# Table loads issued by GpSimd, smaller X tiles and regrouped products in an edge-gated graph kernel

## Chip, core and metric

The kernel runs on one NeuronCore of a Trainium2 chip. The metric is device time in microseconds (us) of one execution; the time of a kernel is the median of its runs.

## What is computed

One gated graph layer over 16 batches of 1024 nodes with 256 features and a sparse 1024 x 1024 adjacency matrix (0.4% of the pairs, made symmetric, and the diagonal):

```python
pre_u = einsum('bud,dk->buk', h, W1[:d]);  pre_v = einsum('bvd,dk->bvk', h, W1[d:])
S = sigmoid(einsum('buvk,ko->buvo', relu(pre_u[:,:,None] + pre_v[:,None] + b1), W2)[...,0] + b2[0])
a_t = einsum('buv,bud->bvd', S * A, h);     m_t = einsum('uv,bud->bvd', A, h) * h
z   = beta1*h + beta2*(a_t @ Wa + ba) + beta3*(m_t @ Wm + bm)
```

## The kernel before

**Pieces and blocks.** Only the edges are worked on. The 1024 targets v are cut into 8 tiles of 128, the 16 batches into 4 groups of 4; a *block* k is one target tile of one group, 32 blocks in all. A block has two windows of 64 targets, and each window five *pieces* of 128 edges: 320 pieces, numbered n, ten to a block. The place of a piece in its block is s = n mod 10. For each piece GpSimd (POOL) gathers 128 rows of 8 KB from a table in DRAM (`fetch`, L474): the first half of a row is pre_u of one source node for four batches, the second half its h. The gathers go into eight places (`fetched0` to `fetched7`); a place is free again when the piece's last product has read it, so about eight gathers are the whole lead.

**One step n** of the main loop (L844) does, in the order in which each engine gets its instructions: evict the last pair of pieces from PSUM (`pair_end`, L634, tile `ev`); expand the target side of piece n+2 by a product with a 0/1 matrix (`expand`, L573, tile `pc`, reading `X`); the block's own products (`products`); in even steps the aggregation of pieces n-2 and n-1 (`aggregate`, L626, tile `acc`), the two gathers that this frees room for, and some small gathers of edge weights (`val`, L348); then VectorE (DVE) adds (`add`, L603) and makes the gate's dot products (`gate`, L610), and ScalarE (ACT) makes the sigmoid (L613) and the weighted edge matrix `left` (L581, L617).

**Products of a block**, by step s: `halves` of the next block (L400 with w_v, L437 to L444; the target side X in a high and a low part); `turn_over` (L648, `LT`: the aggregated rows are transposed, once per window, and multiplied by h in `times_h`, L665); `block_end` of the block before (L676, L684, L688; `z`, L691, written out at L693); and `rows` (L400 with w_u, L416, `tab`, written to the table at L420), which makes table rows for a later group, in the steps listed by `plan` (L748 to L750).

**Loads.** `load_hT` (L389) loads the transposed h of one tile and group (512 KB) and is issued by SyncE (SP) 14 steps ahead (`AHEAD`) of its first use, if one of the 10 (later 13) places for it is free. `copy_h` (L394) copies h of the same rows, 512 KB from DRAM to the table in DRAM; in the main loop ACT issues it. SP also issues the writes of `tab` and `z`. During the first ten blocks the edge lists of tiles 4 to 7 are still being made (`lists`, L214 to L341): POOL loads a 512 KB tile `key` (L216) and DVE works on it from L224 on, in small instructions between the others; `start_list` says in which step each list begins, and `piece_of` how many steps pass after its load.

**What sets the order.** The program's own order is kept on each engine (a manual schedule); the framework puts in semaphore waits. DMAs share eight completion semaphores for those of SP and ACT together (shown as DMAHW0 to DMAHW7) and eight for those of POOL (DMASW0 to DMASW7), used in turn: a DMA waits on its engine until the DMA before it on the same semaphore has landed.

Of the kernel before, what the change touches and what calls it, by code (L numbers as in the profile page):

```python
# [17 lines left out]
def kernel(  # L18
# [364 lines left out]
    def drop_hT(k):  # L383
        hT_free.append(hTs.pop(k))
# [22 lines left out]
    def rows(k, tab=None):  # L407

        g, nt = k
        for h in range(2):  # L410
            step = yield
            c = slice(2 * h * D, (2 * h + 2) * D)
            p = small("p")
            half_product(p, hTs[k], w_u, h, False)
            t = big.tile([P, 2 * D], FP, name=f"tab{h}", bufs=1) if tab is None else tab[:, c]
            nc.scalar.copy(t, p)  # L416
            if h == 1 and k in again:
                drop_hT(k)
            if tab is None:
                after(step + 1, lambda t=t, c=c: nc.sync.dma_start(table[g][nt * P:(nt + 1) * P, c], t))  # L420
        if tab is not None:
            after(step + 1, lambda: nc.sync.dma_start(table[g][nt * P:(nt + 1) * P, :GD], tab))
# [5 lines left out]
    def halves(k):  # L428
        X = cuts[k] = big.tile([P, NW, GD], FR, name="X")
        low = one.tile([P, GD], FP, name="low")  # L430
        for h in range(2):
            step = yield
            c = slice(2 * h * D, (2 * h + 2) * D)
            p = small("p")
            add_row(p, b1_p)
            half_product(p, hTs[order[k]], w_v, h, True)
            nc.scalar.copy(X[:, 0, c], p)  # L437
            nc.scalar.copy(low[:, c], p)
        after(step + (2 if k else 1), lambda: nc.vector.tensor_tensor(low, low, X[:, 0, :].bitcast(FP), ALU.subtract))
        yield  # L440
        nc.scalar.copy(X[W:, 1, :], X[W:, 0, :].bitcast(FP))
        for w in range(NW):
            yield
            nc.scalar.copy(X[(1 - w) * W:(2 - w) * W, w, :], low[w * W:(w + 1) * W])  # L444
# [19 lines left out]
    EVS = 4  # L464
# [103 lines left out]
    def expand(n):  # L568
        k, g, vt, w, j = where(n)
        pcs[n] = psc.tile([P, GD], FP, name="pc")  # L570
        for h in range(2):
            c = slice(2 * h * D, (2 * h + 2) * D)
            nc.tensor.matmul(pcs[n][:, c], marks[n // TW][:, j * P:(j + 1) * P], cuts[k][:, w, c],  # L573
                             start=True, stop=True)
# [95 lines left out]
    def block_end(k):  # L670
# [6 lines left out]
        for h in range(2):  # L677
            for i, wt in ((1, w_a), (0, w_m)):
                step = yield
                if i:  # L680
                    pz = small("pz")
                    for bb in range(2):
                        for e in range(DC):
                            nc.tensor.matmul(pz[:, bb * D + e * P:bb * D + (e + 1) * P], hT[:, 2 * h + bb, e, :], ident,  # L684
                                             is_transpose=True, start=(bb == 0 and e == 0), stop=True, skip_group_check=True)
                for bb in range(2):
                    for c in range(DC):
                        nc.tensor.matmul(pz[:, bb * D:(bb + 1) * D], LT[:, 2 * h + bb, i if bb else 1 - i, c, :], wt[:, c, :],  # L688
                                         start=False, stop=True, skip_group_check=True)
            o = big.tile([P, 2, D], FP, name=f"z{h}", bufs=1)  # L690
# [5 lines left out]
        drop_hT(order[k])  # L696
# [42 lines left out]
    start_list = dict(zip((7, 18, 48, 86), range(EARLY, NT)))  # L739
# [8 lines left out]
    plan(turn[NT:], ((2, 4), (8, 9), (10, 14), (19, 20), (24, 29), (30, 34), (39, 40), (44, 48)))  # L748
    for g, first in ((2, 60), (3, 140)):
        plan([(g, vt) for vt in range(NT)], ((first + 9 + 10 * i, first + 14 + 10 * i) for i in range(NT)))  # L750
# [21 lines left out]
    def products(n, k, s):  # L772
# [238 lines left out]
```

## Time and profile before

| | |
|---|---|
| median of 3 runs | 1106.19 us (1101.87 to 1107.52) |
| the profiled execution, own time | 1100.63 us |
| its span, first to last instruction | 1098.8 us |
| busy of the span | PE 91%, DVE 89%, ACT 79%, POOL 42% |
| DMA: moved, mean rate | 375.00 MB, 341 GB/s |
| share of the 16 DMA engines by queue | POOL's (q0) 72.2%, SP's (q1) 16.7%, ACT's (q10) 3.6% |
| mean granted TensorE clock | 0.958 |

A row of the profile names a line of the kernel, an engine, and what is written and read (out<-in). "Idle before" is the time an engine stood still ahead of an instruction, and what ended it. The DMA share of a stretch is the time that packets took, as a share of 16 engines; packets of several queues can overlap on one engine, so it may be a little over 1.

### The profile page before, as it was taken

The numbers are of one execution on the slowest core, as the hardware profiler recorded it, in microseconds if no ns is written. First come the engines' busy times: TensorE is split into PE (matmuls) and PEld (weight loads), VectorE is DVE, ScalarE is ACT, GpSimd is POOL, SyncE is SP. The second block draws the span as 40 slices with busy tenths as digits, with TensorE's granted clock in tenths as the row PEclk, the third lists the DMA queues.
The fourth block names the chain that finished last, engine by engine and source line by source line (L and its number), as shares of the span: only waits on it lengthen the run. The fifth ranks groups of instructions, "written<-read, shape, count | busy, mean of one in ns | idle before, by whom it ended". The sixth has DMA issues, their size and how long they took to land.

```text
span 1098.8 us, 21630 instructions
## 1 busy us (share of the span) xinstructions
PE 997.1 (91%) x6377; PEld 721.6 (66%) x6377; DVE 977.8 (89%) x3392; ACT 869.7 (79%) x2712; POOL 466.9 (42%) x471
## 2 busy tenths in 40 slices
PE   7858889697999989996999997999999999999986
PEld 6635667475677757774777775777776666666654
DVE  8859989597999899995999996999999999999992
ACT  3437778486888978884988877988989999999972
POOL 2756766455357324651334332433333333333320
PEclk9968989799999999997999998999999999999998
DMA  9999999689999989998999998999999999999981
GB/s 285 329 383 349 367 329 368 221 305 350 348 342 357 380 330 369 379 383 289 360 377 377 395 361 287 377 365 387 353 363 360 364 347 343 357 365 349 359 311 32
DMA packets 133118, 375.00 MB, mean 341 GB/s; under 512 B 17680, under 2 KB 87824, under 8 KB 96784
## 3 DMA queue, kind: packets, MB, share of 16 engines
q0 software_dynamic: 50544, 301.16, 72.2%
q1 hardware_dynamic: 69152, 59.26, 16.7%
q10 hardware_dynamic: 13296, 13.11, 3.6%
q8 instruction: 53, 0.87, 0.3%
q14 instruction: 73, 0.60, 0.1%
HBM read 377.53 MB, written 50.33 MB: 389 GB/s over the span
## 4 chain that ended last, share of the span: by engine, by line
PE 52%; DMA 22%; DVE 11%; ACT 11%; issue 3%; POOL 1%; ACTq 0%; POOLq 0%; DVEq 0%; SPq 0%
PE misc L688 13%; PE misc L400 13%; PE acc L626 11%; PE pc L573 9%; DMA table<-tab 8%; DMA hT<-in_xT_dram 5%; DVE fetched L610 4%; DMA fetched<-table,uidx 4%; DVE fetched L603 3%; DMA key<-in_adjT_dram 3%; PE misc L648 3%; ACT left L617 2%; ACT LT L650 2%; PE misc L684 2%; ACT gt L613 1%
## 5 line engine op out<-in xcount | busy, mean ns | idle before, releaser
L474 POOL DMA_INDIRECT fetched<-table,uidx x320 | 344.7, 1077 | 538.7 <-PE acc L626 404.4
L610 DVE SCALAR_TENSOR_TENSOR fetched<-fetched,w_b 128x256 f32<-128x256 f32 x1280 | 474.4, 416 | 6.9 <-ACT gt L613 6.9
L603 DVE TENSOR_TENSOR fetched<-fetched,pc 128x1024 f32<-128x1024 f32 x320 | 387.6, 1211 | 67.7 <-PE pc L573 49.3
L617 ACT ACTIVATE left<-left,gt 128x16 f32<-128x16 f32 x1280 | 285.1, 296 | 0.0
L573 PE MATMUL pc<-X,mark 128*128 128x512 f32 x640 | 248.0, 470 | 29.3 <-DVE fetched L603 29.3
L626 PE MATMUL acc<-fetched,left 128*32 128x256 f32 x2560 | 228.4, 397 | 48.4 <-ACT left L617 28.7
L626 PEld LDWEIGHTS acc<-fetched,left 128*32 128x32 f32 x2560 | 93.4, 110 | 153.8 <-ACT left L617 71.6
L573 PEld LDWEIGHTS pc<-X,mark 128*128 128x128 f32 x640 | 107.2, 193 | 108.7 <-issue 51.8
L613 ACT ACTIVATE gt<-sc,b_b 128x4 f32<-128x4 f32 x320 | 96.3, 301 | 59.8 <-DVE fetched L610 47.2
L400 PE MATMUL misc<-w_u,hT 128*128 128x256 f32 x512 | 124.7, 392 | 6.1 <-DMA hT<-in_xT_dram 6.1
L400 PE MATMUL misc<-w_v,hT 128*128 128x256 f32 x512 | 122.6, 383 | 0.0
L688 PE MATMUL misc<-w_a,LT 128*128 128x256 f32 x496 | 121.4, 389 | 0.0
L688 PE MATMUL misc<-w_m,LT 128*128 128x256 f32 x496 | 117.4, 379 | 0.0
L400 PEld LDWEIGHTS misc<-w_u,hT 128*128 128x128 f32 x512 | 101.0, 198 | 22.5 <-DMA w_u<-in_W_dram 6.0
L400 PEld LDWEIGHTS misc<-w_v,hT 128*128 128x128 f32 x512 | 98.3, 192 | 15.9
L688 PEld LDWEIGHTS misc<-w_m,LT 128*128 128x128 f32 x496 | 93.7, 189 | 15.0 <-issue 0.4
L348 POOL DMA_INDIRECT val<-in_adjT_dram,vidx x80 | 88.4, 1105 | 31.8 <-issue 17.8
L688 PEld LDWEIGHTS misc<-w_a,LT 128*128 128x128 f32 x496 | 92.9, 198 | 10.7
L581 ACT ACTIVATE left<-onehot,val 128x32 f32<-128x32 bf16 x320 | 99.3, 310 | 0.0
L610 DVE DVE_READ_ACCUMULATOR fetched<-fetched,w_b 128x1 f32 x1280 | 98.9, 77 | 0.0
L634 ACT COPY ev<-acc 128x512 f32<-128x512 f32 x160 | 90.8, 568 | 5.7 <-PE acc L626 5.7
L437 ACT CAST X<-misc 128x512 fp32r<-128x512 f32 x64 | 37.4, 585 | 66.4 <-PE misc L400 66.2
(134 smaller groups left out, 936.3 us busy)
## 6 DMA issues: line engine op xcount, KB each, us to landing
hT<-in_xT_dram SPq DMA_DIRECT2D x35, 512.0 KB, 17.4
out_dram<-z SPq DMA_DIRECT2D x62, 256.0 KB, 10.5
table<-in_x_dram ACTq DMA_DIRECT2D x24, 512.0 KB, 15.3
table<-tab SPq DMA_DIRECT2D x48, 256.0 KB, 15.5
fetched<-table,uidx POOLq DMA_INDIRECT x320, 9.7
table<-in_x_dram SPq DMA_DIRECT2D x8, 512.0 KB, 11.8
table<-fetched SPq DMA_DIRECT2D x8, 512.0 KB, 11.9
fetched<-in_adjT_dram SPq DMA_DIRECT2D x4, 512.0 KB
```

Source lines behind the costliest of these rows:

```text
L348: nc.gpsimd.indirect_dma_start(out=val[:, i, j:j + 1], out_offset=None, in_=adj_flat, in_offset=bass.IndirectOffsetOnAxis(ap=vidx[:, i, j: ...
L400: nc.tensor.matmul(p[:, bb * D:(bb + 1) * D], hT[:, 2 * h + bb, i, :], wt[:, i, :], start=(i == 0 and not begun), stop=(i == DC - 1), skip ...
L474: nc.gpsimd.indirect_dma_start(out=fetched[at_slot[n]], out_offset=None, in_=table[g], in_offset=bass.IndirectOffsetOnAxis(ap=uidx[:, vt * ...
L573: nc.tensor.matmul(pcs[n][:, c], marks[n // TW][:, j * P:(j + 1) * P], cuts[k][:, w, c], start=True, stop=True)
L581: nc.scalar.activation(lefts[n][:, 1::GB, :], onehot[:, vt * NW + w, j, :].unsqueeze(1).to_broadcast([P, GB // 2, V]), AF.Copy, scale=val[ ...
L603: nc.vector.tensor_tensor(t, t, pcs.pop(n), ALU.add)
L610: nc.vector.scalar_tensor_tensor(t[:, b, :], t[:, b, :], 0.0, w2_b, ALU.max, ALU.mult, accum_out=sc[:, b:b + 1])
L613: nc.scalar.activation(gt, sc, AF.Sigmoid, bias=b2_b)
L617: nc.scalar.activation(lefts[n][:, 2 * b, :], lefts[n][:, 1 + b // 2 * GB, :], AF.Copy, scale=gt[:, b:b + 1])
L626: nc.tensor.matmul(accs[i][b * 2 * V:(b + 1) * 2 * V, r, :], left[:, 2 * b - b % 2:2 * b - b % 2 + 2].rearrange("p k v -> p (k v)"), f[:, ...
L634: nc.scalar.copy(evs[i], accs.pop(i))
L688: nc.tensor.matmul(pz[:, bb * D:(bb + 1) * D], LT[:, 2 * h + bb, i if bb else 1 - i, c, :], wt[:, c, :], start=False, stop=True, skip_grou ...
```

## The change

- **Issuers.** In the main loop the loads of hT and the copies of h are issued by POOL (in `made_rows`), no longer by SP and ACT. 26 loads and 24 copies move; the loads ahead of the main loop stay where they were.
- **X** is two tiles of 64 targets' use each (`X[0]`, `X[1]`, 4 KB a partition), out of three places, instead of one tile of 8 KB in two places. The second is taken when it is first written.
- **tab** has two places for each half of the rows instead of one; **z** three places for both halves together instead of one each; **ev** three places instead of four (`EVS`).
- **Places of hT** are given back one step later (`drop_hT` with a step).
- **Steps.** Rows of groups 2 and 3 are made at s = 9 and s = 0 instead of 9 and 4, and some of group 1 move by one step; `block_end` runs in steps 4 to 7 instead of 5 to 8, and makes the product with w_a first, then the transposes of h and the product with w_m into the same PSUM tile; the first `turn_over` of a block is at s = 8 instead of 9.
- **Lists.** A list's work begins eight steps after its load instead of four, and lists 5 to 7 start four steps sooner (14, 44, 82 instead of 18, 48, 86).

```diff
-            t = big.tile([P, 2 * D], FP, name=f"tab{h}", bufs=1) if tab is None else tab[:, c]
+            t = big.tile([P, 2 * D], FP, name=f"tab{h}") if tab is None else tab[:, c]
...
-        X = cuts[k] = big.tile([P, NW, GD], FR, name="X")
+        X = cuts[k] = [big.tile([P, GD], FR, name="X", bufs=3)]
...
-        nc.scalar.copy(X[W:, 1, :], X[W:, 0, :].bitcast(FP))
+        X.append(big.tile([P, GD], FR, name="X", bufs=3))
+        nc.scalar.copy(X[1][W:], X[0][W:].bitcast(FP))
...
-    EVS = 4
+    EVS = 3
...
-            r[1:] = said not in ("slot", "step"), n + {"load": 4, "wait": 2, "slot": 1, "step": 1}.get(said, 0)
+            r[1:] = said not in ("slot", "step"), n + {"load": 8, "wait": 2, "slot": 1, "step": 1}.get(said, 0)
...
                 if i:
                     pz = small("pz")
+                else:
                     for bb in range(2):
                         for e in range(DC):
...
-                                             is_transpose=True, start=(bb == 0 and e == 0), stop=True, skip_group_check=True)
+                                             is_transpose=True, start=False, stop=True, skip_group_check=True)
...
-            o = big.tile([P, 2, D], FP, name=f"z{h}", bufs=1)
+            o = big.tile([P, 2, D], FP, name="z", bufs=3)
...
-        drop_hT(order[k])
+        drop_hT(order[k], step + 1)
...
-    start_list = dict(zip((7, 18, 48, 86), range(EARLY, NT)))
+    start_list = dict(zip((7, 14, 44, 82), range(EARLY, NT)))
...
-        plan([(g, vt) for vt in range(NT)], ((first + 9 + 10 * i, first + 14 + 10 * i) for i in range(NT)))
+        plan([(g, vt) for vt in range(NT)], ((first + 9 + 10 * i, first + 10 + 10 * i) for i in range(NT)))
...
-                load_hT(k)
+                load_hT(k, nc.gpsimd)
             if k not in begun:
-                copy_h(k)
+                copy_h(k, nc.gpsimd)
...
-        if s in (4, 5, 6, 7, 8) and 0 < k < BS:
+        if s in (4, 5, 6, 7) and 0 < k < BS:
             if s == 4:
                 ending = block_end(k - 1)
                 next(ending)
+                go(ending, n)
             go(ending, n)
...
-            if s == 9 and k < BS - 1 or s == 8 and k == BS - 1:
+            if s == 8 and k < BS:
```

On ACT, before, step 125 (s = 5 of block 12; `table_62` is the table of group 2): the copy of h, L394, stands between the work on X and the gate of the step, and waits for the DMA before it on its semaphore.

```order
L634 COPY ev_5797<-acc 128x512 [waits PE_49]
L506 CAST mark<-whose 128x640 [waits DMASW7_49,DMASW0_49]
L441 CAST X<-X 64x1024
L394 DMA table_62<-in_x_dram 128x4x256 [waits DMAHW4_49]
L613 ACTIVATE gt<-sc,b_b 128x4 [waits DVE_49]
L581 ACTIVATE left<-onehot,val 128x2x16 [waits DMASW5_49]
L617 ACTIVATE left<-left,gt 128x16 [waits Activation_49]
```

The same step on ACT now: the copy is gone, and the eviction of z has come one step sooner.

```order
L639 COPY ev_5816<-acc 128x512 [waits PE_49]
L511 CAST mark<-whose 128x640 [waits DMASW1_49,DMASW0_49]
L446 CAST X<-X 64x1024
L697 COPY z<-misc 128x512 [waits DMAHW4_49,PE_49]
L618 ACTIVATE gt<-sc,b_b 128x4 [waits DVE_49]
L586 ACTIVATE left<-onehot,val 128x2x16 [waits DMASW7_49]
L622 ACTIVATE left<-left,gt 128x16 [waits Activation_49]
```

On POOL, before, at the turn to group 2 (`fetched_162` to `fetched_169` are the eight places): gathers alone.

```order
L474 DMA fetched_169<-table_61,uidx 128x2048 [waits DMASW6_49,DVE_49,PE_49]
L474 DMA fetched_162<-table_62,uidx 128x2048 [waits DMAHW2_49,DMAHW3_49,DMAHW1_49,DMAHW4_49,DMAHW0_49,DMAHW5_49,DMASW7_49,DMAHW7_49,DVE_49,PE_49]
L474 DMA fetched_163<-table_62,uidx 128x2048 [waits DMASW0_49,DVE_49,PE_49]
L474 DMA fetched_164<-table_62,uidx 128x2048 [waits DMASW1_49,DVE_49,PE_49]
L474 DMA fetched_165<-table_62,uidx 128x2048 [waits DMASW2_49,DVE_49,PE_49]
```

The same place on POOL now: a load of hT and a copy of h stand between two pairs of gathers, as once in each block that makes rows.

```order
L479 DMA fetched_169<-table_61,uidx 128x2048 [waits DMASW4_49,DVE_49,PE_49]
L479 DMA fetched_162<-table_62,uidx 128x2048 [waits DMAHW2_49,DMAHW1_49,DMAHW5_49,DMASW5_49,DMAHW6_49,DVE_49,PE_49]
L479 DMA fetched_163<-table_62,uidx 128x2048 [waits DMASW6_49,DVE_49,PE_49]
L393 DMA hT_183<-in_xT_dram 128x8x128 [waits DMASW7_49,Activation_49]
L398 DMA table_63<-in_x_dram 128x4x256 [waits DMASW0_49]
L479 DMA fetched_164<-table_62,uidx 128x2048 [waits DMASW1_49,DVE_49,PE_49]
L479 DMA fetched_165<-table_62,uidx 128x2048 [waits DMASW2_49,DVE_49,PE_49]
```

On PE, before, from s = 8 to s = 0 of a block that makes rows: the first half of the rows (L400) and the ten transposes of `turn_over` (L648) stand in one step, between two expansions (L573).

```order
L626 MATMUL acc<-fetched_167,left 32x256 x4
L573 MATMUL pc<-X,mark 128x512 x2
L400 MATMUL misc<-w_u,hT_178 128x256 x4
L648 MATMUL misc<-ident,ev_8281 128x8x16 x2
L648 MATMUL misc<-ident,ev_8350 128x8x16 x2
L648 MATMUL misc<-ident,ev_8424 128x8x16
L648 MATMUL misc<-ident,ev_8281 128x8x16 x2
L648 MATMUL misc<-ident,ev_8350 128x8x16 x2
L648 MATMUL misc<-ident,ev_8424 128x8x16
L573 MATMUL pc<-X,mark 128x512 x2
L626 MATMUL acc<-fetched_168,left 32x256 x4
L626 MATMUL acc<-fetched_169,left 32x256 x4
```

The same place on PE now: the transposes stand a step sooner, ahead of the aggregation of s = 8, and the two halves of the rows follow in s = 9 and s = 0.

```order
L653 MATMUL misc<-ident,ev_8376 128x8x16 x2
L653 MATMUL misc<-ident,ev_8451 128x8x16
L631 MATMUL acc<-fetched_166,left 32x256 x4
L631 MATMUL acc<-fetched_167,left 32x256 x4
L578 MATMUL pc<-X,mark 128x512 x2
L404 MATMUL misc<-w_u,hT_178 128x256 x4
L578 MATMUL pc<-X,mark 128x512 x2
L404 MATMUL misc<-w_u,hT_178 128x256 x4
L631 MATMUL acc<-fetched_168,left 32x256 x4
L631 MATMUL acc<-fetched_169,left 32x256 x4
L578 MATMUL pc<-X,mark 128x512 x2
```

More of the change, by code (lines that the diff above doesn't have):

```diff
@@ L381, with drop_hT @@
     hT_free = hT_places(hts, NH)
-    def drop_hT(k):
-        hT_free.append(hTs.pop(k))
+    def drop_hT(k, step=None):
+        t = hTs.pop(k)
+        if step is None:
+            hT_free.append(t)
+        else:
+            after(step, lambda: hT_free.append(t))
     def load_hT(k, engine=nc.sync):
@@ L688, in block_end @@
                         nc.tensor.matmul(pz[:, bb * D:(bb + 1) * D], LT[:, 2 * h + bb, i if bb else 1 - i, c, :], wt[:, c, :],
[L689 to L690 removed]
+                                         start=(i == 1 and bb == 0 and c == 0), stop=True, skip_group_check=True)
+            o = big.tile([P, 2, D], FP, name="z", bufs=3)
             nc.scalar.copy(o.rearrange("p b d -> p (b d)"), pz)
```

13 lines of the change are left out of this document (7 added, 6 removed).

## The prediction

> **What bounds the kernel now.** I read the stages first: busy times in the list stage (blocks 0 to 6), in the two stages with rows (blocks 7 to 17 and 18 to 22), and in the late blocks without rows. Columns: stretch, length, busy PE, PEld, DVE, ACT, POOL, granted clock, DMA share, GB/s.
>
> ```profile
> 64.00:319.00 255.00, 219.39 (x1344) 157.96 (x1345) 221.80 (x797) 186.35 (x578) 140.26 (x141) 0.91 0.92 335
> 319.00:674.00 355.00, 331.20 (x2122) 242.11 (x2121) 314.92 (x1079) 294.98 (x924) 145.79 (x137) 0.97 0.96 360
> 674.00:823.00 149.00, 147.78 (x973) 109.19 (x972) 139.26 (x465) 132.36 (x417) 54.99 (x50) 1.00 0.96 359
> 823.00:1046.00 223.00, 215.04 (x1432) 151.20 (x1431) 221.72 (x747) 206.75 (x662) 83.05 (x80) 1.00 0.94 355
> ```
>
> Late, DVE works 221.7 of 223 us: the change takes nothing from DVE, so I leave that stage and the tail as they are. In the three stages before, DVE stands still 759 - 676 = 83 us. Who it, and ACT and POOL with it, waited for (columns: total us, times, longest; ACT's and POOL's rows over the whole span, DVE's from 64 to 823 us):
>
> ```profile
> ACT tab L416 <- DMA table<-tab: 19.9, 4, 11.9
> ACT gt L613 <- DMA hT<-in_xT_dram: 10.4, 1, 10.4
> DVE fetched L603 <- PE pc L573: 48.0, 37, 10.4
> DVE key L224 <- DMA key<-in_adjT_dram: 17.0, 3, 6.8
> DVE fetched L603 <- DMA fetched<-table,uidx: 10.1, 9, 2.8
> POOL fetched L474 <- PE acc L626: 404.4, 144, 10.5
> ```
>
> So three things stop the core: ACT waits for an old `tab` write, ACT waits once behind its copy of h, DVE waits for a list's key. The 48.0 us that DVE waits for PE are partly their echo, as the timeline shows at the copy of step 125:
>
> ```profile
> 497.65 9.49 SPq L420 DMA_DIRECT2D table<-tab  x1
> 507.55 0.56 ACTq L394 DMA_DIRECT2D table<-in_x_dram  x1
> 508.16 0.30 ACT L613 ACTIVATE gt<-sc,b_b 128x4 f32<-128x4 f32 x1 [10.38 <-DMA hT<-in_xT_dram]
> 508.92 1.65 PE L626 MATMUL acc<-fetched,left 128*32 128x256 f32 x8 [9.86 <-ACT left L617]
> 511.76 1.22 DVE L603 TENSOR_TENSOR fetched<-fetched,pc 128x1024 f32<-128x1024 f32 x1 [10.39 <-PE pc L573]
> ```
>
> ACT's copy waits for an hT load to land, the gate behind it waits 10.38, PE 9.86, DVE 10.39 us; SP meanwhile needs 9.49 us to issue one write. What is late is thus SP's DMA queue. Its transfers, from 319 to 674 us and then from 840 to 1040 us (queue rows: packets, MB, share of 16 engines; others: count, KB each, median us to landing):
>
> ```profile
> q0 software_dynamic: 16727, 102.44, 74.9%
> q1 hardware_dynamic: 24638, 19.30, 16.4%
> q10 hardware_dynamic: 5808, 5.77, 4.7%
> hT<-in_xT_dram SPq DMA_DIRECT2D x15, 512.0 KB, 21.9
> table<-in_x_dram ACTq DMA_DIRECT2D x11, 512.0 KB, 16.6
> out_dram<-z SPq DMA_DIRECT2D x21, 256.0 KB, 19.0
> fetched<-table,uidx POOLq DMA_INDIRECT x110, 9.5
> ```
> ```profile
> q0 software_dynamic: 10394, 67.00, 88.4%
> q1 hardware_dynamic: 3808, 3.67, 5.2%
> out_dram<-z SPq DMA_DIRECT2D x14, 256.0 KB, 9.4
> ```
>
> A write of z lands in 9.4 us when it has the queue to itself, in 19.0 us when hT loads share it. Engine time of each: z 5.2% x 200 / 14 = 0.74 us; an hT load (16.4% x 355 - 43 x 0.74) / 15 = 1.76 us, taking a tab write to cost what z does; a copy 4.7% x 355 / 11 = 1.52 us; a gather 74.9% x 355 / 110 = 2.42 us. A load of 1.76 us that lands after 21.9 us is not slow, it waits its turn. The program's slices make an hT load of 1024 runs of 512 B, 64 for each engine.
>
> The Trainium skill, "DMA: Bandwidth & Descriptors", section "Queues, rings and completion order", says that an engine takes turns between its queues a packet at a time. The rows agree: a gather packet of 8 KB costs 88.4% x 200 x 16 / (67.00 MB / 8 KB) = 0.35 us, so 64 turns behind one each make about 24 us against 21.9. By this rule the pile-up ends once the loads leave SP's queue, and the sum is the one below; if only bytes counted, it would stay and the stalls at tab and copy would only move, the third rival.
>
> **How far the rest can follow.** PE is nearly full in the blocks with rows. Ten steps there, by the expansions' starts, with three of the five aggregations:
>
> ```profile
> 572.22 0.73 PE L573 MATMUL pc<-X,mark 128*128 128x512 f32 x2
> 577.25 1.07 PE L626 MATMUL acc<-fetched,left 128*32 128x256 f32 x16
> 578.25 0.73 PE L573 MATMUL pc<-X,mark 128*128 128x512 f32 x2
> 582.20 0.64 PE L626 MATMUL acc<-fetched,left 128*32 128x256 f32 x8
> 584.22 0.73 PE L573 MATMUL pc<-X,mark 128*128 128x512 f32 x2
> 588.40 1.49 PE L626 MATMUL acc<-fetched,left 128*32 128x256 f32 x16
> 589.83 0.73 PE L573 MATMUL pc<-X,mark 128*128 128x512 f32 x2
> 601.98 0.73 PE L573 MATMUL pc<-X,mark 128*128 128x512 f32 x2
> ```
>
> 601.98 - 572.22 = 29.76 us a block. An aggregation holds PE 1.00 us when its operands are ready (577.25 to 578.25), but 2.02 and 1.43 us in the two after the crowded step 9. Without that, 29.76 - 1.02 - 0.43 = 28.3 us.
>
> The DMA engines are as full. Two stretches of the same stage, both without a stall:
>
> ```profile
> 575.00:600.00 25.00, 24.76 (x163) 18.32 (x162) 23.49 (x80) 22.06 (x69) 8.81 (x8) 1.00 0.98 373
> 600.00:625.00 25.00, 24.75 (x170) 18.06 (x172) 23.08 (x78) 21.99 (x74) 8.73 (x8) 1.00 1.01 401
> ```
>
> I take 0.99 as a share that can be held. The work of the three stages is 0.92 x 255 + 0.96 x 355 + 0.96 x 149 = 718 us, which at 0.99 takes 726 us of the 759: **the DMA engines leave 33 us**, less than half of DVE's 83.
>
> **The change part by part.**
>
> ```profile
> L474 POOL DMA_INDIRECT fetched<-table,uidx x320 | 344.7, 1077 | 538.7 <-PE acc L626 404.4 <-DVE fetched L603 53.4 <-DVE fetched L610 26.5
> L389 POOL DMA_DIRECT2D hT<-in_xT_dram x1 | 1.0, 970 | 0.0
> ```
>
> - *26 loads and 24 copies to POOL.* POOL pays about 50 x 0.97 = 48 us, in odd steps, when no gather is due; it covers that with the 404 us that it waits for PE. If that cover were gone, a pair of gathers would start some 2 us late. On the DMA engines the price of a load lies between what it costs now, 1.76 us, and a gather's rate, 2.42 us for 102.44 / 110 = 0.93 MB, so 1.37 us for 0.52 MB; a copy between 1.52 and 1.37. Saved: 0 to 26 x 0.39 + 24 x 0.15 = 14 us; I take half, **-7**. ACT sheds 24 issues of 0.56 us and the 10.4 us wait; behind that copy stood the gate and, through it, PE and DVE.
> - *What now queues behind them.* Gathers wait behind a load and a copy, 3.3 us of engine time, once a block. The 9 late gathers (10.1 us) show little reserve, so this lies between 0 and 26 x 1.76 + 24 x 1.52 = 82 us. I take 0 beyond the DMA bound, which holds this work already. At the start two copies, a load and a copy now precede the ninth gather: 0 to 3 x 1.52 + 1.76 = 6.3 us, but the first eight gathers no longer share the engines with them: **+2**.
> - *tab in two places.* Takes away up to 19.9 us of ACT's waits: a place is reused after some 20 steps instead of 10. In the bound.
> - *Key eight steps ahead.* Takes away up to 17.0 us; next late would be the list's small DMAs on POOL, behind gathers. In the bound.
> - *Rows and block_end spread.* PE could give 1.45 us a block; in the 16 blocks with rows DMA binds first, so 0 on top.
> - *X, z, ev, places of hT.* X[1] is taken at s = 5, three steps after its place's last reader; a z place is reused after 12 to 18 steps instead of 10; a fourth ev is not needed once `turn_over` runs before the fourth pair is evicted; hT comes back one step later with 14 steps of lead. No wait row names any of them: 0, with 3 either way for the range.
>
> Sum: 1098.8 - 33 - 7 + 2 = 1061 us of span. The profiled execution took 1.8 us more than its span (1100.63) and lies 5.6 below the median of the runs; with 1.8, and 3 of a possible 0 to 5.6, **1065 us**.
>
> **Rivals.**
> - *DMA does not bind* (17%). For it: gathers land in 9.5 us in a stage with a share of 0.96, so no line of gathers has built up there, and 401 GB/s were moved for 25 us where the stage's mean is 360. Then DVE and PE bind: 222 + 10 late gathers, 318 (DVE's 315 and a little; PE 11 x 28.3 = 311) and 5 x 28.3 = 142, together 692 instead of 759: -67, span 1032, time 1036.
> - *Gathers late behind the loads: slower* (8%). If the adds see the 82 us of moved engine time in full, even the -67 turn into +15: 1121 us. It decides from 67/82 of it. Against: in most blocks DMA did this work between the same gathers before.
> - *The change doesn't relieve the queue: no change* (8%). POOL's own eight semaphores are shared with loads and copies now; a late load then holds POOL as it held ACT, and four stalls of 10 us (the longest above are 11.9 and 10.4) come back there: 1065 + 40, so 1098 to 1108.
> - *Half of the stalls stay* (7%): 1085 to 1098.
>
> **How the numbers follow.** The likeliest case has 60%, its own range 1048 to 1085. The range 1030 to 1092 leaves out the slower case, the unchanged one and a rest of 3%. About 0.5%, or 5.5 us, is what a measurement of this kernel can tell from no change. Faster: 60 + 17 + 7 = 84%; within: 8%; slower: 8%.
>
> **What would show it.** Right: no wait of ACT on a DMA of tab or hT, none of DVE on key; z landing near 10 us in all stages; DMA shares of 0.98 and more in the first three stages; DVE waiting for gathers instead of PE in blocks with rows, which stay near 29 us; late blocks unchanged. Wrong: blocks with rows at 28.3 us or less (DMA was no bound), or POOL idle before gathers on DMAs of its own, with DVE late by more than 40 us on gathers.

## The result, and the profile after

The changed kernel takes 1089.34 us (median of 12 runs, 1080.16 to 1099.12) where the kernel before takes 1102.71 us (12 runs on the same chip): ratio 0.987, 95% interval 0.984 to 0.991. It is faster, by 13 us; 41 were forecast. On two other chips the ratio came out at 0.987 again (0.980 to 0.994 and 0.983 to 0.991). The execution profiled with the first measurement was a disturbed one, so the profile is read from the changed kernel's second measurement, an execution of 1081.11 us with a span of 1079.3 on a chip where before takes 1092.4.

The four stages of the changed kernel, in the columns of the prediction's first fence:

```profile
64.00:319.00 255.00, 230.24 (x1428) 165.60 (x1427) 234.60 (x837) 197.97 (x615) 164.19 (x165) 0.95 0.95 354
319.00:674.00 355.00, 339.48 (x2185) 245.45 (x2183) 319.94 (x1091) 302.93 (x944) 165.63 (x164) 1.00 0.96 367
674.00:823.00 149.00, 145.06 (x936) 105.58 (x935) 137.97 (x460) 131.29 (x415) 56.08 (x56) 1.00 0.95 358
823.00:1046.00 223.00, 215.03 (x1435) 151.76 (x1434) 222.69 (x753) 207.45 (x663) 85.73 (x80) 0.99 0.95 357
```

The DMA share rose in the first stage (0.92 to 0.95), stood still in the second and fell in the third, where 0.98 and more was forecast. Late, DVE is as full as before. The waits have changed in kind (rows over the whole span; the last one, of DVE on PE, from 319 to 823 us):

```profile
POOL fetched L479 <- PE acc L631: 259.5, 94, 6.3
DVE fetched L608 <- DMA fetched<-table,uidx: 60.3, 51, 5.1
DVE fetched L608 <- PE pc L578: 1.6, 1, 1.6
```

No row of ACT on a DMA of tab or hT and none of DVE on a key is left: the stops (single waits of 5 us and more) at tab, behind the copy and at the keys are gone. In their place stand 51 waits of DVE for a gather, 1.2 us each, where there had been 13 of 11.6 us in all. The queues changed with them (319 to 674 us, columns as in the prediction):

```profile
q0 software_dynamic: 20874, 118.37, 86.5%
q1 hardware_dynamic: 9174, 11.57, 9.0%
hT<-in_xT_dram POOLq DMA_DIRECT2D x15, 512.0 KB, 13.1
out_dram<-z SPq DMA_DIRECT2D x22, 256.0 KB, 9.3
fetched<-table,uidx POOLq DMA_INDIRECT x113, 13.4
```

SP's queue is empty enough now: z lands after 9.3 us instead of 19.0, an hT load after 13.1 instead of 21.9. But a gather takes 13.4 us instead of 9.5.

Where the time went is seen best by blocks. I take the start of the add of steps 0, 70 and 230 in each trace, which gives blocks 0 to 6 (the list stage), 7 to 22 (those with rows) and the rest to the end of the span; the time ahead of step 0, 60 to 65 us, is in no column. Single profiles are good to some 5 us here: two kernels below that are the same up to step 60, e10 and e11, differ by 5.3 us in blocks 0 to 5. The profile of before is from another chip than that of the changed kernel; e2, which takes as long as before, ran on the changed kernel's chip.

| kernel | ratio to before | blocks 0-6 | 7-22 | rest |
|---|---|---|---|---|
| before | 1 | 255.5 | 503.7 | 275.7 |
| changed | 0.987 | 247.1 | 500.0 | 271.5 |
| e1 loads on SP, copies on ACT | 0.986 | 233.9 | 502.7 | 271.0 |
| e2 before, with issuers of the change | 0.998 | 252.9 | 503.8 | 274.6 |
| e3 copies on SP | 0.980 | 239.1 | 497.7 | 274.2 |
| e4 16 blocks without writes of z | 0.972 | 248.7 | 487.1 | 269.9 |
| e5 those writes twice | 1.001 | 250.2 | 517.6 | 270.6 |
| e6 before, with keys of the change | 1.003 | 255.5 | 503.8 | 278.5 |
| e7 one place for each half of tab | 0.982 | 244.8 | 501.1 | 271.0 |
| e8 copies 7 steps after their load | 0.983 | 248.7 | 499.7 | 269.9 |
| e9 as e1, one place for each half of tab | 0.990 | 245.8 | 508.1 | 273.2 |
| e10 copies on SP, loads on SP to step 60 | 0.980 | 239.7 | 499.8 | 273.5 |
| e11 as e10 to step 60, then as e8 | 0.980 | 245.4 | 501.6 | 269.2 |
| e12 as e7, nine places for gathers | 0.982 | 250.0 | 498.3 | 269.2 |
| e13 as e12, issuers as e10 | 0.980 | 247.4 | 498.0 | 269.3 |
| e14 keys as before | 0.992 | 251.9 | 506.1 | 272.1 |

The column of blocks 7 to 22 is the finding: whoever issues what, with stops of 10 us or with none, these 16 blocks take 498 to 508 us as long as they move the same bytes. Of the 19.5 us between the profiles of before and changed, 11.6 are gained when block 7 starts (319.4 and 307.8 us); the 3.7 and 4.2 us behind that are less than single profiles resolve.

### The profile page after: what moved, and what is told of

Same layout as the page of the kernel before. It is cut to its first block, busy times and chain, and to the rows that moved or that the text cites. A ratio compares the mean times of both kernels' runs of the same rounds, so it can differ in the third digit from the quotient of the medians.

```text
span 1097.3 us, 21612 instructions
## 1 busy us (share of the span) xinstructions
PE 1007.6 (92%) x6377; PEld 727.3 (66%) x6377; DVE 980.1 (89%) x3392; ACT 873.4 (80%) x2712; POOL 504.6 (46%) x521
## 2 busy tenths in 40 slices
DMA packets 100606, 375.00 MB, mean 342 GB/s; under 512 B 17680, under 2 KB 48912, under 8 KB 64272
## 4 chain that ended last, share of the span: by engine, by line
PE 30%; DVE 25%; DMA 20%; ACT 11%; issue 9%; POOL 2%; another core or an unknown queue 1%; POOLq 0%; DVEq 0%
DMA fetched<-table,uidx 18%; DVE fetched L615 12%; DVE fetched L608 9%; PE misc L404 9%; PE acc L631 6%; PE pc L578 5%; PE misc L694 5%; ACT left L622 3%; PE misc L653 2%; DMA hT<-in_xT_dram 2%; DVE low L443 1%; ACT X L449 1%; ACT gt L618 1%; ACT ev L639 1%
## 5 line engine op out<-in xcount | busy, mean ns | idle before, releaser
L631 PE MATMUL acc<-fetched,left 128*32 128x256 f32 x2560 | 230.8, 394 | 38.3 <-ACT left L622 18.7
L631 PEld LDWEIGHTS acc<-fetched,left 128*32 128x32 f32 x2560 | 98.6, 109 | 135.3 <-ACT left L622 54.0
L404 PE MATMUL misc<-w_v,hT 128*128 128x256 f32 x512 | 125.8, 390 | 0.0
L694 PE MATMUL misc<-w_a,LT 128*128 128x256 f32 x496 | 117.7, 380 | 0.0
L404 PEld LDWEIGHTS misc<-w_v,hT 128*128 128x128 f32 x512 | 101.0, 197 | 17.0
L348 POOL DMA_INDIRECT val<-in_adjT_dram,vidx x80 | 84.6, 1057 | 32.2 <-issue 22.0
L694 PEld LDWEIGHTS misc<-w_m,LT 128*128 128x128 f32 x496 | 91.0, 194 | 10.1
L653 PE MATMUL misc<-ident,ev 128*128 128x128 f32 x642 | 83.8, 276 | 4.8 <-issue 4.8
```

The costliest lines, as they stand in the source:

```text
L404: nc.tensor.matmul(p[:, bb * D:(bb + 1) * D], hT[:, 2 * h + bb, i, :], wt[:, i, :], start=(i == 0 and not begun), stop=(i == DC - 1), skip ...
L631: nc.tensor.matmul(accs[i][b * 2 * V:(b + 1) * 2 * V, r, :], left[:, 2 * b - b % 2:2 * b - b % 2 + 2].rearrange("p k v -> p (k v)"), f[:, ...
L653: nc.tensor.matmul(pt[:, :, FROM[j]:FROM[j] + V], evs[i][:, r, c * P:(c + 1) * P], ident, is_transpose=True, start=(j == of[0]), stop=True ...
```

## The experiments

Each run was made beside runs of the kernel before on its chip, whose median was between 1092 and 1103 us; so ratios are compared. Three theories stood at the start. **T1**: gathers stand in POOL's queue behind the load and the copy, and that order costs some 3.3 us a block. **T2**: the DMA engines are the bound in the blocks with rows, whoever issues. **T3**: the issuers alone carry the gain.

**Changed again (e0).** No edit.

> The changed kernel again, unaltered, to have an undisturbed profile of it. Both theories: about 1089 us (ratio 0.987). Theory 1 (queue order): in each block with rows the adds at s = 2 to 4 come 3 to 3.6 us late in sum, waiting for gathers, and the DMA share stays at 0.96 or less. Theory 2 (the DMA engines are the bound): the share is 0.98 or more in the blocks with rows.

Measured: 1081.11 us, ratio 0.987; the rows above. The share of 0.98 that T2 asked for isn't there, and the late adds that T1 asked for are: in blocks 18 and 19 those of s = 2 to 4 wait 2.8 and 3.3 us for gathers.

**Issuers undone (e1).**

```diff
-                load_hT(k, nc.gpsimd)
+                load_hT(k)
...
-                copy_h(k, nc.gpsimd)
+                copy_h(k)
```

> The changed kernel with the loads of hT issued by SP and the copies of h by ACT again; all else as changed. Theory 1 (gathers stand behind a load and a copy in POOL's queue, about 3.3 us a block with rows): blocks with rows fall to 28.3 to 29.8 us, a stall or two at ACT's copies come back, time 1055 to 1075 us. Theory 2 (the DMA engines are the bound, whoever issues): 1085 to 1092 us. Theory 3 (the new issuers alone carry the gain): about 1100 us.

Measured: 1076.49 us, ratio 0.986 (0.977 to 0.995), which the measurement doesn't tell from the changed kernel's 0.987. From 319 to 674 us its SP queue is worse than before's:

```profile
hT<-in_xT_dram SPq DMA_DIRECT2D x15, 512.0 KB, 35.0
out_dram<-z SPq DMA_DIRECT2D x22, 256.0 KB, 21.7
table<-tab SPq DMA_DIRECT2D x22, 256.0 KB, 23.6
```

ACT stops for it:

```profile
ACT gt L618 <- DMA hT<-in_xT_dram: 8.5, 1, 8.5
ACT z L697 <- DMA out_dram<-z: 6.0, 1, 6.0
```

and yet blocks 7 to 22, here and in the changed kernel, last equally long (e1 first, then changed):

```profile
298.50:801.20 502.70, 475.12 (x3102) 352.54 (x3104) 454.88 (x1541) 426.53 (x1343) 194.61 (x186) 0.98 0.97 362
```
```profile
307.80:807.80 500.00, 481.40 (x3102) 349.33 (x3104) 453.90 (x1542) 430.59 (x1343) 221.96 (x218) 1.00 0.96 365
```

Stops of 6 to 9 us are made up for by blocks of 29 to 30 us between them; the changed kernel has no stop and 31 us a block. No theory had the total. T1 missed it by little, but its blocks of 28.3 to 29.8 us are 31.4 on the mean; T2's total was 9 us too high, but its statement, that the issuers don't matter, holds in these blocks.

**Issuers alone (e2): before, with the loads and copies issued by POOL.**

```diff
-                load_hT(k)
+                load_hT(k, nc.gpsimd)
...
-                copy_h(k)
+                copy_h(k, nc.gpsimd)
```

> The kernel before with the new issuers alone: loads of hT and copies of h by POOL. Theory 1: the stalls of ACT go, but the late gathers come on top of the crowded step 9: 1105 to 1125 us. Theory 2: 1085 to 1095 us. Theory 3: about 1089 us.

Measured: 1091.96 us, ratio 0.998 (0.995 to 1.002). The issuers alone change nothing in the whole, and T3 falls. What they do inside the list stage comes below.

**Copies on SyncE (e3), loads still on POOL.**

```diff
-                copy_h(k, nc.gpsimd)
+                copy_h(k, nc.sync)
```

> The changed kernel with the copies of h issued by SP (nobody computes there), the loads of hT still by POOL. Theory 1: the gathers stand behind the load alone, some 1.5 us less in each of 24 blocks: 1050 to 1068 us. Theory 2: 1085 to 1092 us. Theory 3: 1089 to 1095 us.

Measured: 1074.27 us, ratio 0.980 (0.973 to 0.987), outside all three forecasts. The gain on the changed kernel lies in blocks 0 to 6 (239.1 us against 247.1); this comes back below.

**Bytes taken away and added (e4, e5).** z uses SP's queue, which holds no gather, load or copy in the changed kernel's main loop. So its bytes tell the rate of the DMA from the order of POOL's queue. e4 leaves 16 blocks of z unwritten; e5 writes them a second time, to a scratch tensor (`twice`).

```diff
-            after(step + 1, lambda o=o, b=b: nc.sync.dma_start(
-                out[b:b + 2, vt * P:(vt + 1) * P, :].rearrange("b p d -> p b d"), o))
+            if not 6 <= k <= 21:
+                after(step + 1, lambda o=o, b=b: nc.sync.dma_start(
+                    out[b:b + 2, vt * P:(vt + 1) * P, :].rearrange("b p d -> p b d"), o))
```

> The changed kernel without the 32 writes of z of the blocks that end in blocks 7 to 22 (z is still computed and copied out of PSUM, the output lacks those 16 blocks). z goes through SP's queue, which no gather, load or copy uses. T2 (the DMA engines are full in blocks 7 to 22, which last 500 us in the changed kernel): each write costs them 0.74 us, so those blocks lose 24 us or nearly that: 476 to 482 us, and the whole 1057 to 1065 where the changed kernel takes 1081. T1 (gathers wait their turn behind a load and a copy in POOL's queue; the engines have time left): the gathers' queue is as long as before, 495 to 500 us and 1076 to 1082. A third theory, that PE or DVE holds these blocks at 31 us: no change either.

```diff
+            if 6 <= k <= 21:
+                after(step + 1, lambda o=o, i=2 * k + h: nc.sync.dma_start(twice[i].rearrange("b p d -> p b d"), o))
```

> The changed kernel with those 32 writes of z made twice, the second time to a scratch tensor in DRAM, in the same shape and by the same queue of SP. T2: 24 us of engine time more, blocks 7 to 22 take 520 to 524 us, the whole 1101 to 1106. T1, and a theory by which PE or DVE holds these blocks: 500 to 504 us, the whole 1081 to 1085.

Measured: ratios 0.972 (0.965 to 0.979) and 1.001 (0.997 to 1.005). Blocks 7 to 22, e4 and then e5:

```profile
310.80:797.90 487.10, 477.02 (x3093) 349.44 (x3092) 453.85 (x1540) 428.09 (x1339) 222.32 (x218) 1.00 0.95 359
```
```profile
311.50:829.10 517.60, 484.49 (x3115) 351.34 (x3113) 455.29 (x1542) 432.73 (x1347) 224.57 (x220) 0.99 0.96 370
```

Work that no compute engine waits for takes 12.9 us out of these blocks and puts 17.6 us in (14 and 16 us beside e7, on the same chip). PE, DVE and ACT work nearly the same. So the DMA's rate bounds these blocks, as T2 says; whether that is the DMA engines' own or that of the memory behind them, no run here tells. But 32 writes of 0.74 us would be 24 us, so only half to three quarters of the engine time is felt. A possible reason is the shape of a block. Block 18 of the changed kernel in quarters:

```profile
654.40:662.50 8.10, 8.10 (x53) 5.91 (x48) 5.69 (x22) 7.18 (x26) 3.90 (x4) 1.00 0.99 385
662.50:670.00 7.50, 6.88 (x44) 4.71 (x43) 6.62 (x20) 5.08 (x18) 2.29 (x3) 1.00 0.94 370
670.00:677.50 7.50, 7.50 (x47) 5.71 (x48) 7.50 (x28) 6.83 (x20) 3.76 (x4) 1.00 0.86 326
677.50:685.50 8.00, 7.81 (x60) 5.50 (x59) 8.00 (x29) 7.85 (x25) 2.11 (x2) 1.00 1.02 376
```

In the first quarter the engines are at 0.99 and DVE waits (5.69 of 8.10 us busy); in the third DVE has 7.50 of 7.50 us to do and the engines run down to 0.86 (the lull); in the last both are full. So the bound seems to change hands within a block. POOL's DMA issues at that place, and two of DVE's adds:

```profile
673.18 0.99 POOL L479 DMA_INDIRECT fetched<-table,uidx  x1 [4.44 <-DVE fetched L608]
674.47 0.99 POOL L479 DMA_INDIRECT fetched<-table,uidx  x1 [0.30 <-issue]
675.46 0.96 POOL L393 DMA_DIRECT2D hT<-in_xT_dram  x1
676.41 0.83 POOL L398 DMA_DIRECT2D table<-in_x_dram  x1
679.33 1.08 POOL L479 DMA_INDIRECT fetched<-table,uidx  x1 [2.09 <-DVE fetched L608]
687.97 1.21 DVE L608 TENSOR_TENSOR fetched<-fetched,pc 128x1024 f32<-128x1024 f32 x1
694.13 1.22 DVE L608 TENSOR_TENSOR fetched<-fetched,pc 128x1024 f32<-128x1024 f32 x1 [2.97 <-DMA fetched<-table,uidx]
```

The gather issued at 679.33, behind the load and the copy, is that of piece 192 and serves the add of 694.13, which waited 2.97 us for it.

**The copy put into the lull (e8).** If the lull in the third quarter is what is lost, the copy belongs there:

```diff
-                copy_h(k, nc.gpsimd)
+                after(max(n + 7, 0), lambda k=k: copy_h(k, nc.gpsimd))
```

> The changed kernel with each copy of x issued 7 steps after its load instead of right behind it, on GpSimd still. Two readings of the 31 us blocks. Full all the time (the engines have no room anywhere in a block): moving 1.4 us of transfers changes nothing, blocks 7 to 22 stay at 500 us and the ratio to before at 0.987. Full in part of a block (in blocks 18 and 19 of the changed kernel the DMA share is 0.99, 0.94, 0.86, 1.02 and 0.99, 0.99, 0.78, 1.02 over four quarters; load and copy come right behind the third quarter, and the gathers behind them are the late ones): the copy now falls into the third quarter, the first gathers of the next block come 1.4 us earlier in the 14 blocks with a copy, up to 20 us less, 480 to 492 us, ratio 0.970 to 0.981.

Measured: 1082.81 us, ratio 0.983 (0.979 to 0.986). Block 18 again:

```profile
655.50:663.23 7.73, 7.73 (x47) 5.99 (x47) 6.21 (x20) 6.68 (x24) 3.48 (x4) 1.00 0.97 376
663.23:670.95 7.72, 7.27 (x45) 5.03 (x44) 6.88 (x24) 5.69 (x19) 3.27 (x4) 1.00 0.95 348
670.95:678.67 7.72, 7.72 (x48) 5.68 (x46) 7.72 (x25) 7.01 (x19) 3.00 (x3) 1.00 0.94 369
678.67:686.40 7.73, 7.51 (x59) 5.14 (x58) 7.21 (x28) 7.61 (x25) 2.43 (x3) 1.00 1.01 374
```

The lull is filled (0.94 for 0.86), and the block is 30.9 us long instead of 31.1; blocks 7 to 22 take 499.7 us. Of the two readings the one with room in a block, 480 to 492 us, failed: a filled lull wins no time. The rates show it better than the shares: the block moves 365 GB/s as changed and 367 with the copy in the lull (means of its four quarters).

**Keys alone, tab alone, keys undone (e6, e7, e9, e14).** Which part carries the list stage? e6 is before with the lists' start and lead of the change:

```diff
-            r[1:] = said not in ("slot", "step"), n + {"load": 4, "wait": 2, "slot": 1, "step": 1}.get(said, 0)
+            r[1:] = said not in ("slot", "step"), n + {"load": 8, "wait": 2, "slot": 1, "step": 1}.get(said, 0)
...
-    start_list = dict(zip((7, 18, 48, 86), range(EARLY, NT)))
+    start_list = dict(zip((7, 14, 44, 82), range(EARLY, NT)))
```

> The kernel before with one part of the change: three lists start four steps earlier and every list waits eight steps instead of four after its load. If the gain of the changed kernel is made of the stalls that it takes away one by one: block 5 loses its step of 9.3 us (key 5.5 us late) and one block after it a wait of 6.8 us; 10 to 14 us less over the whole where the wait isn't paid back by full DMA engines, and about 6 if only the one in the list stage (blocks 0 to 6) counts, so 1079 to 1087 where before takes 1092. T2 says 6: blocks 7 to 22 together keep their 504 us. If a stall removed here only lets another wait come (the queue of SP is unchanged): 1090 to 1094.

Measured: ratio 1.003 (0.999 to 1.007). No wait for a key is left, and nothing is won: block 5 still takes 38.2 us (39.8 before), and ACT's waits for tab were 19.9 us and are 23.1 here.

```profile
ACT tab L416 <- DMA table<-tab: 23.1, 4, 9.8
```

e7 and e9 give each half of the table rows one place again (`bufs=1`), e7 with loads and copies on POOL, e9 with loads on SP and copies on ACT.

```diff
-            t = big.tile([P, 2 * D], FP, name=f"tab{h}") if tab is None else tab[:, c]
+            t = big.tile([P, 2 * D], FP, name=f"tab{h}", bufs=1) if tab is None else tab[:, c]
```

> The changed kernel with one place for each half of a block's table rows, as before, instead of two. If it is the second place that took away ACT's waits for a written tab (12.6 us in blocks 0 to 6, one of them 11.9 us in block 3): block 3 gets its long step back, 7 to 10 us more, 1088 to 1091 where the changed kernel takes 1081. If it is the queue (hT loads no longer share SP's queue, so a write of tab lands in 8.2 us instead of 11.1): no such wait, 1080 to 1083.

> Loads on SyncE and copies on ScalarE as before the change, one place for each half of the table rows as before; the rest as in the changed kernel. The second place of tab did nothing where loads went by GpSimd's queue (1080.5, no long step in block 3). If it is worth something only behind a piled-up SP queue: block 3 gets its step of 11 us back, 7 to 10 us more than with two places: ratio 0.993 to 0.996 instead of 0.986. If the other moved parts already prevent that wait: 0.984 to 0.988.

Measured: e7 1080.49 us, 0.982 (0.974 to 0.991), no wait of ACT for a write of tab anywhere; e9 1091.89 us, 0.990 (0.987 to 0.993) and so between its two forecasts, with

```profile
ACT tab L420 <- DMA table<-tab: 30.3, 3, 15.2
```

all three in blocks 7 to 22 and not, as one reading had it, in block 3. So in these blocks ACT waits for a tab write only where there is one place and SP's queue is full of hT loads: a second place (e1) and moving the loads away (e7) cure the same stop. What it costs is not resolved, as the ratios of e9 and e1 overlap (0.990 and 0.986). In block 3 the stop is gone even so: the block takes 32.7 us in e9, where it took 41.1 before and 40.2 in e6. So neither the second place nor the issuers are needed there, and the keys alone don't do it. The moved steps, X, z, ev and the places of hT are left, and none of these was run alone.

e14 undoes the lead of the keys in the changed kernel.

> The changed kernel with the lists started and waited for as before (eight steps become four, three lists start four steps later). The lead of the keys alone moved before by nothing (ratio 1.003), yet 17.0 us of waits for keys stood in the profile. If the waits for keys are covered by gathers that would be late anyway: ratio 0.982 to 0.988 as the changed kernel. If they cost once the wait for tab is gone: block 5 longer by 6 us, ratio 0.989 to 0.994.

Measured: 1092.78 us, 0.992 (0.990 to 0.995), 0.5% more than the changed kernel had on other chips, with

```profile
DVE key L224 <- DMA key<-in_adjT_dram: 15.0, 3, 7.3
```

The longest, 7.3 us, is in block 9, which takes 40.0 us here and 34.7 in the changed kernel; block 5, where I expected it, is 3 us longer. So the keys' lead is worth nothing while tab stops ACT, and perhaps 5 us once it doesn't; the intervals of the two ratios touch.

**Nine places for gathers (e12, e13).** A rival to the engines' rate was the loop itself: eight places, a gather that lands after 13.4 us instead of 9.5. In the memory of the second tab place (tab has one place again, as in e7) and of the lists, a ninth place from step 110:

```diff
             hT_free.extend(hT_places(more, MORE, NH))
+            fetched.append(more.tile([P, 2 * GD], FP, name=f"fetched{NF}"))
+            nc.gpsimd.memset(fetched[NF], 0.0)
+            free.append(NF)
```

> The changed kernel with one place for each half of the table rows (which changed nothing), and in the memory won a ninth place for a gather from step 110 on, so from block 11. What holds blocks 12 to 21 (315.5 us in the changed kernel, 313.8 with one tab place) at 31 us? If it is the loop through eight places (a gather lands 13.1 us after its issue where it took 9.5, and its place can't be filled sooner): a ninth gives each gather 3 us more, the late ones (2.6 to 3.1 us a block) come in time, 283 to 295 us, ratio to before 0.955 to 0.968. If it is the rate of the DMA engines: gathers are issued 3 us sooner and land 3 us later, 310 to 316 us, ratio 0.980 to 0.988.

> The same with all copies on SyncE and the loads on SyncE up to step 60. If the loop of places binds: another 5 us below the run with nine places alone, ratio 0.950 to 0.965. If the engines bind: 0.977 to 0.982, as with eight places.

Measured: 1081.16 us, 0.982 (0.977 to 0.986), and 1079.73 us, 0.980 (0.976 to 0.984). Blocks 7 to 22 of e12:

```profile
310.90:809.20 498.30, 480.46 (x3098) 351.24 (x3096) 453.23 (x1540) 428.54 (x1342) 226.31 (x221) 0.99 0.96 369
```

In blocks 18 and 19 a gather is issued 15 to 19 us ahead of its add instead of 12 to 17, a block still takes 31 us, and the late add is that of s = 3 instead of s = 2. The late gathers were issued sooner and landed later, 17 us after their issue instead of 14 to 15. So the number of places is not the bound.

**Which issuer, in the list stage (e10, e11, and on one chip e15, e16).** e10 has copies on SP throughout and loads on SP up to step 60; e11 the same until step 60, and then the copies as in e8 (the second diff, against e10).

```diff
-                load_hT(k, nc.gpsimd)
+                load_hT(k, nc.gpsimd if n >= 60 else nc.sync)
...
-                copy_h(k, nc.gpsimd)
+                copy_h(k, nc.sync)
```

> The changed kernel with all copies on SyncE, and the loads on SyncE in blocks 0 to 5 and on GpSimd from step 60. Blocks 0 to 6 ended at 307.8 us with both on GpSimd, 303.1 with copies on SyncE, 298.5 with neither on GpSimd; blocks 7 to 22 took 500.0, 497.7 and 502.7 us. If a load or copy in GpSimd's queue costs the list stage what these say, block 7 starts at 298 to 300, and the rest is as with copies on SyncE: 5 us less than that one, ratio 0.973 to 0.978 (1072 where before takes 1098.8). If what is won in blocks 0 to 6 is paid back later: 0.980.

```diff
-                copy_h(k, nc.sync)
+                if n < 60:
+                    copy_h(k, nc.sync)
+                else:
+                    after(n + 7, lambda k=k: copy_h(k, nc.gpsimd))
```

> As the one with loads on SyncE until step 60, but the copies from step 60 on go to GpSimd, 7 steps behind their load. If the lull takes them: blocks 7 to 22 at 480 to 492 us and block 7 at 298 to 300: ratio 0.960 to 0.972. If the engines are full throughout: 0.975 to 0.980.

Measured: 1079.96 us, 0.980 (0.977 to 0.983), and 1081.22 us, 0.980 (0.978 to 0.983). e11's copies in the lull did again nothing. Block 7 starts at 303.4 and 308.6 us in them, and not at 298 to 300 as I had expected. The three first blocks took 115.8 to 121.1 us in the nine runs in which POOL issues the copies there, and 107.3 to 116.6 us in the nine in which it doesn't (e15 and e16 are counted in). To tell it from the chips, both kernels on one:

> The changed kernel once more, to stand on one chip with the next one. Copies on GpSimd cost blocks 0 to 2 some 6 us: in eight kernels with them these blocks took 115.8 to 121.1 us, in eight without 108.0 to 116.6. By that this run has 116 to 121 us there, and a ratio to before of 0.982 to 0.988.

> The kernel with copies on SyncE and loads on SyncE up to step 60, beside the changed kernel. If the copies' place in GpSimd's queue costs what the blocks 0 to 2 say: 108 to 114 us there and 5 to 7 us below the changed kernel, ratio 0.977 to 0.982. If the difference of the ratios measured so far (0.9798 and 0.9872) is only that of chips: within 2 us of it.

Measured: changed 1079.85 us, 0.987 (0.983 to 0.991); e10's kernel 1070.73 us, 0.979 (0.975 to 0.983). Blocks 0 to 2, changed and then e10's kernel, with DVE's waits for gathers there:

```profile
60.50:178.60 118.10, 97.69 (x565) 69.94 (x566) 99.81 (x351) 79.14 (x241) 81.75 (x84) 0.91 0.94 340
...
DVE fetched L608 <- DMA fetched<-table,uidx: 16.3, 8, 5.7
```
```profile
63.10:170.40 107.30, 94.04 (x564) 67.25 (x565) 98.23 (x351) 78.76 (x241) 69.30 (x70) 0.93 0.99 366
...
DVE fetched L608 <- DMA fetched<-table,uidx: 3.5, 4, 1.6
```

DVE works nearly the same, but its gathers are late by 16.3 us against 3.5, and the DMA moves 340 GB/s instead of 366. Part of the difference is only moved: where POOL issues them, 7 copies and 5 loads fall into these blocks instead of 4 and 4, and step 0 starts 2.6 us sooner (60.5 and 63.1). At the end of block 2 the changed kernel is 8.2 us behind, and e10's kernel ends 9 us below it, where 5 to 7 were expected. So at the start loads and copies in front of gathers on POOL cost time, as T1 says; whether by their place in the queue or because POOL issues the gathers later, no run tells.

The same cut at step 30 shows what the parts do in the list stage, each of them one profile:

| kernel | step 0 at | blocks 0-2 | blocks 3-6 | block 7 at |
|---|---|---|---|---|
| before | 63.9 | 111.2 | 144.3 | 319.4 |
| changed | 60.7 | 119.3 | 127.8 | 307.8 |
| e2 issuers alone | 60.4 | 121.0 | 131.8 | 313.3 |
| e1 the rest alone | 64.6 | 108.0 | 126.0 | 298.5 |
| e6 keys alone | 62.5 | 112.7 | 142.8 | 318.0 |

The issuers alone (e2) are not idle, as the unchanged whole would suggest: block 3 loses its stop (32.5 us for 41.1) and blocks 3 to 6 are 12.5 us shorter, but blocks 0 to 2 are 9.8 us longer. The rest alone (e1) makes blocks 3 to 6 18 us shorter and pays nothing at the start. Together they win no more than the rest alone, as both take the stop out of block 3.

## Why the prediction was wrong in size

- **The stops and SP's queue: right, but not what the gain hangs on.** No wait of ACT on tab or hT and none of DVE on a key is left, and z lands in 9.3 us. The prediction weighed the Trainium skill's page "DMA: Bandwidth & Descriptors", section "Queues, rings and completion order", by which queues take turns by packets, against a rule by bytes. The trace agrees with turns by packets: an hT load lands after 13.1 us from POOL's queue, 21.9 and 35.0 us from SP's. It doesn't prove them, as a load from POOL also goes in larger packets (last section). But in e1 SP's queue is as full as before (z lands in 21.7 us) and the ratio is the same, and in e2 the queue is relieved (10.1 us) and nothing is gained. So the gain doesn't need the path that the prediction gave it, and that the direction was right is in this part luck.
- **"The DMA engines leave 33 us": the step that failed.** That the DMA binds was right (e4, e5, e12). The size came from a share of 0.99, read off two stretches of 25 us with 0.98 and 1.01 and taken as one "that can be held". Held over 16 blocks were 0.94 to 0.97 in the kernels above. The terms of 33 and 7, less 2 for the start, made 38 us. Measured: blocks 0 to 22 go from 759.2 to 747.1 us, 12 us, or 15 with the earlier start of step 0; from e2 on the same chip it is 10 us. Had I taken the share that the stage already showed, 0.96, for the one to be held, the term would have been 718 / 0.96 = 748, 11 us. Why no more is held stays open: the lull in the third quarter of a block isn't shown to be the cause, as e8 filled it and won nothing. And engine time is no fixed price that a share could be divided into. e2 moves the same 182 MB as e1 with a share of 0.94 against 0.97, in the same time:

```profile
313.30:817.10 503.80, 479.96 (x3095) 349.17 (x3094) 451.52 (x1540) 431.34 (x1343) 223.01 (x219) 0.99 0.94 361
```

- **The price of loads and copies, -7: right in engine time, not shown in time.** In blocks 7 to 22 the queues' shares went from (rows of before, then of changed)

```profile
q0 software_dynamic: 23743, 147.43, 76.3%
q1 hardware_dynamic: 31761, 25.96, 15.4%
q10 hardware_dynamic: 7392, 7.34, 4.2%
```
```profile
q0 software_dynamic: 28531, 165.33, 86.0%
q1 hardware_dynamic: 13238, 16.71, 9.2%
```

  so 95.9% of 503.7 us became 95.2% of 500.0: 483 to 476 us of engine time. In e2, with the same issuers, it is 0.94 of 503.8, 474 us, and these blocks last as long as before: nothing of it reached the clock there.
- **"0 beyond the DMA bound" for gathers behind loads and copies: right in blocks 7 to 22, wrong at the start.** In blocks 7 to 22 the same time is lost in another shape: 31 us a block without stops for 29 to 30 us with them. At the start +2 was forecast. Step 0 does start sooner, by 3.2 us, but block 2 ends 4.9 us later than before, and 8.2 us later than in e10's kernel on one chip. One sign of being wrong came by half: DVE was late by 60 us on gathers, but POOL waited only 5.7 us for gathers of its own before it issued one.
- **Late blocks unchanged: right. PE's room, X, z, ev and the places of hT worth 0: open.** The late row is as before, and the rest after block 22 is 4 us shorter, which single profiles don't resolve. None of these parts was run alone. In e9 they, the moved steps and the keys together free block 3 without the second place of tab and without the issuers.
- **"Blocks with rows stay near 29 us" and shares of 0.98: wrong**, both by the held share. The rival in which DMA doesn't bind had 318 + 142 = 460 us for these 16 blocks, and it showed nowhere: no kernel that moves all its bytes needed less than 497.7 us.

The gain that the profiles resolve is in blocks 3 to 6, 144.3 us before and 127.8 in the changed kernel, without the stops at tab (block 3) and at a key (block 5). Blocks 0 to 2 gave 4.9 us of it back, with the earlier start counted. Blocks 3 to 6, before and then changed, in the columns of the prediction's first fence:

```profile
175.06:319.38 144.32, 124.83 (x792) 90.06 (x791) 123.69 (x450) 108.56 (x339) 72.08 (x71) 0.93 0.88 320
```
```profile
180.00:307.75 127.75, 122.22 (x793) 88.06 (x793) 124.89 (x450) 108.98 (x339) 77.96 (x78) 1.00 0.96 364
```

Here the engines had room: a share of 0.88 before, which rises to the 0.96 of the later blocks. The granted clock rose as well, from 0.93 to 1.00. No run takes the two apart; PE's own busy time differs by only 2.6 of the 16.5 us.

## What to carry to other kernels

In the blocks of this kernel whose DMA engines were already at 0.96, taking away stops only moved the time. Count the gain by the share that a stage holds as a mean, not by the best 25 us of it, and test the bound by adding a transfer that nobody waits for. Look for the gain in the stages where the share is lower (here 0.88), and keep transfers that can wait away from those that can't. Two edits that cure the same stop, like a second buffer and an emptier queue, are to be counted once. And a part that changes nothing in the whole may win in one stage what it loses in another: cut the trace by stages before calling it idle.

## What the runs showed of the hardware

The 375.00 MB of an execution went from 133118 packets to 100606 by moving loads and copies to POOL (the pages' lines, before and changed):

```profile
DMA packets 133118, 375.00 MB, mean 341 GB/s; under 512 B 17680, under 2 KB 87824, under 8 KB 96784
```
```profile
DMA packets 100606, 375.00 MB, mean 347 GB/s; under 512 B 17680, under 2 KB 48912, under 8 KB 64272
```

With the same slices of the program, GpSimd's queue moved the runs of 512 B and 1 KB in fewer, larger packets. The counts come out exactly: the 38912 packets under 2 KB that are gone are 26 loads of 1024 runs and 24 copies of 512, and the 6400 more of 2 to 8 KB are 128 for each of the 50 transfers, so 4 KB each.

The rate of the blocks that the DMA binds hardly depends on the mix: 359 to 370 GB/s over blocks 7 to 22, with 0.94 to 0.97 of the engines' time, in all the kernels read there.
